# Layer 0 of a graph-attention chain: the sums' products grouped by four chunks, in written order

## The chip, the cores and the metric

The kernel runs on one core of a Trainium2 chip. The metric is the device time of one execution in microseconds (us); lower is better. TensorE multiplies matrices, VectorE and ScalarE work element by element, GpSimd (POOL) does one small reduction here, SyncE (SP) issues transfers. The engines run side by side and wait for each other by semaphores.

## The reference, cut to what matters

Four graph layers follow each other on `x` of 16 images (the batch) with 1024 nodes of 64 features, under one adjacency of 1024 x 1024; each ends in a residual and a layer norm. The change is in layer 0, a graph attention:

```python
def _L0_gnn_ref(h, W, a, adj):
    Wh = jnp.einsum('bni,io->bno', h, W)
    s1 = Wh @ a[:64, 0]
    s2 = Wh @ a[64:, 0]
    e = leaky_relu(s1[:, :, None] + s2[:, None, :], negative_slope=0.2)
    e = e + jnp.where(adj == 0, -1e9, 0.0)[None]
    attention = softmax(e, axis=2)
    h_prime = jnp.einsum('bnm,bmo->bno', attention, Wh)
    return elu(h_prime)
...
x = _layernorm(x + _L0_gnn_ref(x, L0_gnn_W, L0_gnn_a, adj))   # layer 0
x = _layernorm(x + _L1_gnn_ref(...))                          # layer 1: softmax of features over neighbours
x = _layernorm(x + _L2_gnn_ref(x, adj, ...))                  # layer 2: as layer 0, other weights
x = _layernorm(x + _L3_gnn_ref(x, adj, ...))                  # layer 3: four heads and an output head
```

## The kernel before

Layers 0 and 2 share one function, `gat_layer`. With `zero_mean` (layer 2) the features have no mean, 63 of them suffice, and the 64th column of the values is used for the softmax's sums. Layer 0's input isn't normalized, so all 64 columns are taken and the sums need products of their own.

The work on an image `b` is a loop over eight chunks `k` of 128 neighbours. `unit(k)` makes the tile `e` (128 neighbours x 1024 nodes, fp32) on VectorE in one instruction from `G`, `q` and the mask `aT`. `product(k, e)` multiplies on TensorE: two matrix products `y_l` with the values (`vals`, 64 columns each, one for each half of the nodes, side by side in the array), and in layer 0 also the sums `u_l` with `only`, a tile of 32 columns of which one is filled. The sums of two chunks make four products that lie side by side in the array; they are issued after every second chunk. `product` is issued two units behind `unit` (`LAG = 2`).

When an image's eight chunks are done, eight small tasks follow in the time of the next images, placed by slot (image, chunk): `evict` (ScalarE copies `yT`, `ysum` out of PSUM), `project` (TensorE, `po`, L1001 and L1005), `divide` (VectorE L1014 to L1019, then the exponential `m` on ScalarE, L1026), `residual` (VectorE L1031, L1032), `norm` (VectorE, eight `bn_stats`, L1040, and for an odd image the moments), `root`, `shift`, and `store` (ScalarE, eight scaled copies back into `x`, L775). Images go in pairs: `prep_x` (transposes `pxT`, L898), `prep_s` (`ps`, L904), `prep_top` (a maximum over all partitions on POOL), `prep_p`, `prep_G` (`pg` on TensorE, L939, then the exponential `G` on ScalarE, L940, one half of the nodes each) and `prep_v` make ready the next pair.

What sets the order of the instructions differs by layer. `gat_layer` has a flag `ordered`. Where it is true (layer 2), the engines' instructions stand in the order in which the code issues them. Where it is false (layer 0 before the change), a scheduler at build time chooses each engine's order from its own estimates, and may deal a task out between the units around it. [...] The flag is the last argument of the call:

```python
        extra = {(0, 6): [lambda: gat_setup(later["w2"], "l2", True)], (1, 6): [lambda: later["w3"]()]}
        ending = gat_layer(w_0, "l0", False, extra, first, 3, False)
```

`extra` holds setups of layers 2 and 3, which are done on the way through images 0 and 1 (weight transposes `wt`, products `l_pa`, `l_pw`, `pw`, and small copies on VectorE). `ending` are the tasks of the last images, which layer 1 takes over.

## Time and profile before

| what | us |
|---|---|
| median of 3 runs | 2162.24 (2161.66 to 2167.61) |
| the profiled execution, its own time | 2170.64 |
| its span, first to last instruction | 2168.8 |
| TensorE busy in the span | 2047.2 (94%) |
| VectorE busy | 1852.5 (85%) |
| ScalarE busy | 1227.5 (57%) |
| layer 0, first `y_l` to first `px` of layer 1 | 31.2 to 292.6 |
| one pair of images of layer 0, from `ps` to `ps` | 32.43 |
| layer 2, first `ps` to the start of layer 3 | about 471 to 735 |

All durations of single instructions come from the profiled execution. A row of a timeline gives start, length, engine, line, operation, tiles (out<-in), shape and how many instruction records follow each other. An fp32 matrix product leaves two records. The length runs to the modelled end of the last one; the start of the next row is the better measure of what a group costs. A bracket at the end is idle time of the engine just before, and what ended it. The granted clock is the share of TensorE's full clock over the stretch.

### The profile page before, as it was taken

What the parts mean: (1) busy time and instruction counts of PE and PEld (TensorE: products, weight loads), DVE (VectorE), ACT (ScalarE), POOL (GpSimd) and SP (SyncE); (2) the same over time, 40 slices, a digit from 0 to 9 for tenths busy, and PEclk for the clock granted to TensorE, in tenths of its full rate; (3) what the DMA queues carried; (4) which work ended last, traced back from release to release, by engine and by line L of the source; (5) the groups of instructions that cost most, each with busy time, mean ns of one, the idle gap of its engine ahead of it and who ended that gap; (6) DMA issues with size and microseconds to landing.
All of it is one profiled execution on the core that took longest, in us unless ns stands there. A gap on an engine that the chain in (4) does not pass through costs nothing.

```text
span 2168.8 us, 26641 instructions
## 1 busy us (share of the span) xinstructions
PE 2047.2 (94%) x10321; PEld 866.2 (40%) x10321; DVE 1852.5 (85%) x3221; ACT 1227.5 (57%) x1965; POOL 51.0 (2%) x77
## 2 busy tenths in 40 slices
PE   7999979998898899999999999999999999999993
PEld 3333347753433333333333333333333433343331
DVE  5888889978988877798898898889889889888997
ACT  4454556555535666566655665655665665565541
POOL 0000000000000000000000000000000000000001
PEclk8999989988978999999999999999999999999997
DMA  6000000000000200000000000000000000000000
GB/s 162 1 1 1 1 1 1 1 1 1 1 1 1 72 6 1 1 1 6 1 6 5 1 6 1 6 5 1 6 6 1 6 1 6 6 1 6 1 7 15
DMA packets 23656, 18.92 MB, mean 9 GB/s; under 512 B 19361, under 2 KB 19426, under 8 KB 23522
## 3 DMA queue, kind: packets, MB, share of 16 engines
q1 hardware_dynamic: 23218, 17.11, 2.8%
q8 instruction: 83, 1.36, 0.3%
q14 instruction: 51, 0.42, 0.1%
q10 hardware_dynamic: 304, 0.03, 0.0%
HBM read 12.95 MB, written 4.19 MB: 8 GB/s over the span
## 4 chain that ended last, share of the span: by engine, by line
PE 73%; DVE 21%; ACT 4%; issue 1%; DMA 0%; POOL 0%; SPq 0%; POOLq 0%; DVEq 0%; ACTq 0%
PE y L1259 18%; PE s L1247 17%; PE y_l L971 8%; PE s L1344 5%; PE y L1371 4%; DVE e L1252 4%; PE u_l L982 3%; DVE e L959 3%; PE po L1276 3%; PE po L1531 3%; PE po L1005 2%; PE pg L939 2%; PE po L1001 1%; PE ps L904 1%; ACT e L1251 1%
## 5 line engine op out<-in xcount | busy, mean ns | idle before, releaser
L1251 ACT ACTIVATE e<-s,shift 128x1024 f32<-128x1024 f32 x512 | 542.9, 1111 | 243.2 <-PE s L1247 237.8
L1252 DVE TENSOR_TENSOR e<-e,aT 128x1024 f32<-128x1024 f32 x512 | 602.6, 1220 | 87.7 <-ACT e L1251 85.6
L1247 PE MATMUL s<-hT 64*128 64x512 f32 x2048 | 509.9, 612 | 15.5 <-DVE top L1188 8.6
L1259 PE MATMUL y<-e,vals 128*64 128x512 f32 x2048 | 490.6, 601 | 3.2 <-ACT yT L1266 1.3
L959 DVE SCALAR_TENSOR_TENSOR e<-G_l,q,aT 128x1024 f32<-128x1024 f32 x256 | 319.9, 1276 | 20.5 <-ACT G_l L940 12.4
L971 PE MATMUL y_l<-e,vals_l 128*64 128x512 f32 x1024 | 278.8, 660 | 27.9 <-DVE e L959 26.3
L1247 PEld LDWEIGHTS s<-hT 64*128 64x128 f32 x2048 | 182.5, 186 | 256.0 <-issue 170.8
L1259 PEld LDWEIGHTS y<-e,vals 128*64 128x64 f32 x2048 | 131.0, 136 | 330.6 <-issue 258.0
L1349 ACT ACTIVATE e<-s,shift 128x1024 f32<-128x1024 f32 x128 | 141.8, 1113 | 85.1 <-PE s L1344 74.9
L1351 DVE TENSOR_TENSOR me<-e,aT 128x1024 f32<-128x1024 f32 x128 | 155.8, 1220 | 16.8 <-ACT e L1349 16.5
L1362 DVE SCALAR_TENSOR_TENSOR junk<-e,aN 128x1024 bf16<-128x1024 f32 x128 | 155.9, 1218 | 0.2
L1371 PE MATMUL y<-me,h2v 128*64 128x512 f32 x512 | 135.3, 609 | 10.5 <-DVE me L1351 10.4
L1344 PE MATMUL s<-h2T 64*128 64x512 f32 x512 | 136.3, 610 | 4.6 <-DVE h2v L1331 4.4
L971 PEld LDWEIGHTS y_l<-e,vals_l 128*64 128x64 f32 x1024 | 65.3, 146 | 184.9 <-issue 75.4
L1531 PE MATMUL po<-hi,aR 128*128 128x512 f32 x256 | 101.9, 398 | 2.7 <-ACT hi L1516 1.1
L775 ACT ACTIVATE x<-m,bn_shift,bn_rstd 128x64 f32<-128x64 f32 x256 | 88.7, 432 | 23.2 <-DVE bn_shift L766 23.2
L1531 PE MATMUL po<-lo,aR 128*128 128x512 f32 x256 | 99.8, 391 | 0.0
L1306 ACT COPY zT<-pzT 128x1024 f32<-128x1024 f32 x32 | 32.4, 1012 | 78.3 <-PE pzT L1305 78.3
L1276 PEld LDWEIGHTS po<-wb,yT 128*128 128x128 f32 x512 | 62.0, 190 | 34.0 <-issue 21.1
L1276 PE MATMUL po<-wb,yT 128*128 128x130 f32 x512 | 73.8, 287 | 1.3 <-ACT e L1251 1.2
L982 PE MATMUL u_l<-e,only 128*32 128x512 f32 x512 | 72.0, 612 | 0.0
L1344 PEld LDWEIGHTS s<-h2T 64*128 64x128 f32 x512 | 46.6, 186 | 63.7 <-issue 41.4
(214 smaller groups left out, 2019.9 us busy)
## 6 DMA issues: line engine op xcount, KB each, us to landing
adj<-in_adj_dram SPq DMA_DIRECT2D x16, 512.0 KB, 4.4
x<-in_x_dram SPq DMA_DIRECT2D x16, 256.0 KB, 5.0
out_dram<-res SPq DMA_DIRECT2D x16, 256.0 KB, 2.0
wl<-in_L_gnn_Wh_dram SPq DMA_DIRECT2D x2, 64.0 KB, 5.3
wo<-in_L_gnn_Wo_dram SPq DMA_DIRECT2D x1, 64.0 KB, 5.0
l_wd<-in_L_gnn_W_dram ACTq DMA_DIRECT2D x2, 16.0 KB, 4.7
l_wd<-in_L_gnn_W_dram SPq DMA_DIRECT2D x2, 16.0 KB, 2.0
bo<-in_L_gnn_bo_dram SPq DMA_DIRECT2D x1, 32.0 KB, 3.3
```

Source lines behind the costliest of these rows:

```text
L959: nc.vector.scalar_tensor_tensor(e, G[b - b % 2][:, b % 2, :], pq[b - b % 2][1][:, k, b % 2 : b % 2 + 1], aT[:, k, :], ALU.max, ALU.mult,)
L971: nc.tensor.matmul(held["y"][h * D : (h + 1) * D, :], vals[b][:, k, :], e[:, h * HALF : (h + 1) * HALF], start=(k == 0), stop=(k == C - 1),)
L1247: nc.tensor.matmul(s[:, i, :], hT[rows, k * P : (k + 1) * P], hT[rows, cols], start=True, stop=True)
L1251: nc.scalar.activation(e, s, AF.Exp, bias=shifts[b, n])
L1252: nc.vector.tensor_tensor(e, e, bc_mid(aT[:, k, cols], 2), ALU.mult)
L1259: nc.tensor.matmul(held[h][i * D : (i + 1) * D, :], vals[b][:, k, :], e[:, i, :], start=(k == 0), stop=(k == C - 1),)
L1276: nc.tensor.matmul(o[:, j // 2, j % 2, :], held["y"][:, c * P : (c + 1) * P], wb[:, n, :], start=True, stop=True,)
L1344: nc.tensor.matmul(s[:, i, :], hT[rows, (i + k // CH) % 2, k % CH * P : (k % CH + 1) * P], hT[rows, 0, :], start=True, stop=True,)
L1351: nc.vector.tensor_tensor(m, e, aT[:, k, :].rearrange("p (i q) -> p i q", i=2), ALU.mult)
L1362: nc.vector.scalar_tensor_tensor(junk, held.pop(k).rearrange("p i q -> p (i q)"), 1.0, aN[:, k, :], ALU.mult, ALU.mult, accum_out=sums[:, ...
L1371: nc.tensor.matmul(held["o"][h * D : (h + 1) * D, :], vals["out", b][:, k, :], e[:, h, :], start=(k == 0), stop=(k == C - 1),)
L1531: nc.tensor.matmul(po.rearrange("p q k f -> p (q k f)"), aR[:, k, ic * P : (ic + 1) * P], e[:, k].rearrange("p q k f -> p (q k f)"), start ...
```

## The change

In layer 0 alone: the sums' products wait until four chunks' products of values have been issued and then come as a group of eight; tiles `e` have ten buffers in place of seven; the small tasks have other slots (of an even image, `project`, `divide` and `residual` come two slots later, one for `residual`; of the next pair's preparation, `ps` and the second half of `G` come later, behind the sums), and the whole layer is recorded in written order. Layer 2 keeps its slots, and the other layers are untouched. No operation is added or left out.

```diff
-                e = pool.tile([P, N], F32, tag="e", name="e", bufs=7)
+                e = pool.tile([P, N], F32, tag="e", name="e", bufs=7 if zero_mean else 10)
...
-                if not zero_mean:
-                    if k % 2 == 0:
-                        held["e"] = e
-                    else:
-                        for r in range(4):
-                            kk, ee = (k - 1, held["e"]) if r < 2 else (k, e)
-                            h = r % 2
-                            nc.tensor.matmul(
-                                held["t"][r * 32 : (r + 1) * 32, :], only[b][:, kk, :],
-                                ee[:, h * HALF : (h + 1) * HALF], start=(kk < 2), stop=(kk >= C - 2),
-                            )
+                if zero_mean:
+                    return
+
+                held[k] = e
+                for kk in range(k - 3, k + 1) if k % 4 == 3 else ():
+                    ee = held.pop(kk)
+                    for h in range(2):
+                        r = kk % 2 * 2 + h
+                        nc.tensor.matmul(
+                            held["t"][r * 32 : (r + 1) * 32, :], only[b][:, kk, :],
+                            ee[:, h * HALF : (h + 1) * HALF], start=(kk < 2), stop=(kk >= C - 2),
+                        )
...
-            end = (3, 6) if b % 2 == 0 else (3, 2)
-            for task, (t, k) in zip(work[b][2], ((1, 1), (1, 3), (1, 4), (1, 6), (1, 7), (2, 0), (2, 2), end)):
+
+            places = [(1, 1), (1, 3), (1, 4), (1, 6), (1, 7), (2, 0), (2, 2), (3, 2) if b % 2 else (3, 6)]
+            if not zero_mean and b % 2 == 0:
+                places[1:4] = (1, 5), (1, 6), (1, 7)
+            for task, (t, k) in zip(work[b][2], places):
                 at(b + t, k, task)
...
+            if zero_mean:
+                places = (-2, 0), (-2, 1), (-2, 2), (-2, 3), (-1, 1), (-1, 2), (-1, 3), (-1, 4), (0, 4)
+            else:
+                places = (-2, 1), (-2, 1), (-2, 5), (-2, 6), (-1, 0), (-1, 1), (-1, 5), (-1, 4), (0, 4)
+            for task, (t, k) in zip(chain, places):
...
-        ending = gat_layer(w_0, "l0", False, extra, first, 3, False)
+        ending = gat_layer(w_0, "l0", False, extra, first, 3, True)
```

The nine places of the last list belong, in order, to the two halves of `prep_x`, `prep_s`, `prep_top`, `prep_p`, the two halves of `prep_G`, and `prep_v` of both images of the pair.

More of the change, by code (lines that the diff above doesn't have):

```diff
@@ L1072, in gat_layer @@
         for b in range(0, B, 2):
-            chain = [(lambda b=b, h=h: prep_x(b, h), -2, h) for h in range(2)]
-            chain += [(lambda b=b: prep_s(b), -2, 2), (lambda b=b: prep_top(b), -2, 3)]
-            chain += [(lambda b=b: prep_p(b), -1, 1)]
-            chain += [(lambda b=b, h=h: prep_G(b, h), -1, 2 + h) for h in range(2)]
-            chain += [(lambda b=b: prep_v(b), -1, 4), (lambda b=b: prep_v(b + 1), 0, 4)]
-            for task, t, k in chain:
+            chain = [
+                lambda b=b: prep_x(b, 0), lambda b=b: prep_x(b, 1), lambda b=b: prep_s(b), lambda b=b: prep_top(b),
+                lambda b=b: prep_p(b), lambda b=b: prep_G(b, 0), lambda b=b: prep_G(b, 1),
+                lambda b=b: prep_v(b), lambda b=b: prep_v(b + 1),
+            ]
+            if zero_mean:
[3 more added lines that the diff above has]
+            for task, (t, k) in zip(chain, places):
                 if b + t < 0:
```

## Prediction

> **What bounds the kernel now.** I read the page's busy shares first, then the stretches of layer 0 and layer 2, then TensorE's timeline in one pair of images, then ScalarE's and VectorE's. Layer 0's products run from 31.2 us (first y_l) to 292.6 us (first px of layer 1): 261.4 us of the span. The busy times by stretch (stretch, its length, busy us of each engine, granted clock):

> ```profile
> core 0: us, PE busy (x) PEld busy (x) DVE busy (x) ACT busy (x) POOL busy (x), PEclk, DMA share, GB/s
> 138.38:170.80 32.42, 32.42 (x209) 11.96 (x209) 27.14 (x60) 16.80 (x48) 0.35 (x1) 1.00 0.00 1
> 470.00:735.00 265.00, 236.59 (x1168) 104.46 (x1166) 222.95 (x472) 132.91 (x382) 9.34 (x9) 0.83 0.02 7
> ```

> The first row is one pair of images of layer 0: TensorE has no hole in 32.42 us and full clock, VectorE has 5.3 us spare. Five pairs follow each other at 32.43 us. The second is layer 2, recorded in written order already: TensorE is idle 11% of it and its granted clock is 0.83. TensorE's timeline inside the pair (start, length, line, records; two records are one matmul):

> ```profile
> 152.80 1.08 PE L971 MATMUL y_l<-e,vals_l 128*64 128x512 f32 x4
> 153.81 1.13 PE L939 MATMUL pg<-xT_l,l_w 64*128 64x512 f32 x4
> 154.87 1.08 PE L971 MATMUL y_l<-e,vals_l 128*64 128x512 f32 x4
> 155.88 1.06 PE L982 MATMUL u_l<-e,only 128*32 128x512 f32 x8
> 156.87 1.05 PE L1001 MATMUL po<-l_ind,ysum_l 128*128 128x2 f32 x8
> 157.86 1.11 PE L1005 MATMUL po<-l_wd,yT_l 64*128 64x64 f32 x16
> 158.80 1.08 PE L939 MATMUL pg<-xT_l,l_w 64*128 64x512 f32 x4
> 159.81 1.94 PE L971 MATMUL y_l<-e,vals_l 128*64 128x512 f32 x8
> 161.68 1.06 PE L982 MATMUL u_l<-e,only 128*32 128x512 f32 x8
> ```

> From start to start: values of two chunks (y x8) 1.87 us, of one chunk (y x4) 1.01, sums of two chunks (u x8) 1.00. A chunk more in a y group therefore costs 0.86, and cutting a group costs 2 x 1.01 - 1.87 = 0.15. ScalarE at the same place:

> ```profile
> 159.49 1.10 ACT L775 ACTIVATE x<-m,bn_shift,bn_rstd 128x64 f32<-128x64 f32 x3 [3.00 <-DVE bn_shift L766]
> 160.50 1.09 ACT L940 ACTIVATE G_l<-pg,up 128x1024 f32<-128x1024 f32 x1
> 161.50 0.62 ACT L1026 ACTIVATE m<-v 128x512 f32<-128x512 f32 x1
> 162.02 4.41 ACT L775 ACTIVATE x<-m,bn_shift,bn_rstd 128x64 f32<-128x64 f32 x13
> ```

> After G, the exponential of divide (m) goes ahead of 13 of the 16 stores; a store takes 0.33 from start to start. And VectorE:

> ```profile
> 161.63 1.28 DVE L959 SCALAR_TENSOR_TENSOR e<-G_l,q,aT 128x1024 f32<-128x1024 f32 x1 [1.43 <-ACT G_l L940]
> 162.83 0.68 DVE L1031 SCALAR_TENSOR_TENSOR v<-v,x 128x512 f32<-128x512 f32 x1
> 163.43 1.28 DVE L959 SCALAR_TENSOR_TENSOR e<-G_l,q,aT 128x1024 f32<-128x1024 f32 x1
> ```

> The scheduler deals the residual out between the next image's e tiles; an e takes 1.195 from start to start.

> [...]

> **The change, part by part.** Times below are of TensorE unless another engine is named.

> 1. Sums behind four chunks. Before, four chunks cost 2 x (1.867 + 0.996) = 5.73. After: y of four chunks 1.009 + 3 x 0.859 = 3.59, sums 0.996 + 0.859 = 1.86 (that a second set of sums costs 0.86 like a chunk of y is taken; at worst 1.00). Saved 0.285 per four chunks, 32 times: **9.1**.

> 2. Small tasks behind sums. In the built order a pair reads: pxT, y of 2, po, y of 2, u, ps, y of 4, u, pg | y of 4, u, po, pg, y of 4, u. One cut of y is left where there were three, and pxT is whole (its halves took 0.586 and 0.585; some 1.02 together). That is 0.45 per pair over six pairs: **2.7**. A pair without waits is 32.43 - 4 x 0.285 - 0.45 = 30.84. Both together save **11.8**.

> 3. Written order. No instruction is added, and no DMA: SP's and POOL's work keeps its order; only vector, scalar and matrix instructions move. What they stand behind now is the question. At the end of an odd image t (images t-1 and t are a pair) VectorE has: divide of t-1, e(7) of t, residual and norm of t-1, then e(0) of the next pair. ScalarE has: second half of G, **eight stores of image t-3, then** the exponential that this residual needs. G waits for pg, which stands behind po. Nothing of e(0) can start before. From the moment that pg starts:
>  - pg until G can start 1.12 (1.01 to the next group, 0.11 to its end and the signal)
>  - G to the next on ScalarE 1.00
>  - eight stores 8 x 0.333 = 2.66
>  - exponential 0.62, signal 0.04
>  - residual, two steps of 0.685 with 0.04 each 1.45; eight bn_stats 1.02
>  - e(0) 1.28, signal 0.05

>  Behind the waiting residual VectorE has norm and e(0) to e(4), for which y(0) to y(4) wait; behind the late exponential ScalarE has the copies yT and ysum, read by po only two chunks later, so they delay nothing.

>  Sum 9.24. In the meantime TensorE has pg 1.01, y of 4 3.59, u 1.86, pxT 1.02 = 7.48. It then **stands 1.76**. Then y(1) follows e(1), 1.195 behind instead of 0.86 (0.34), and the last y of the next odd group waits 0.15 and is cut (0.15), because norm and moments stand ahead of its e on VectorE. Per pair 2.40: 30.84 + 2.40 = 33.2 against 32.43. Such boundaries: after images 3, 5, 7, 9, 11. After 13 there is no pxT to cover, so 1.02 more. After image 1 no store exists yet: 9.24 - 2.66 = 6.58 is under 7.48, no wait. Sum 5 x 2.40 + 3.42 = **15.4**.

> 4. Setups and ends. Layer 2's weights (wt, l_pa, l_pw) and layer 3's (wt, pw) now stand in order between products; l_pw waits for some ten small vector steps of 0.06 to 0.28, and e(5) behind the copies to wb waits too: 2.0 and 1.5, by adding those steps; from 1 to 5 together. The first four products of image 0 follow e at 1.195: 3 x 0.34 = 1.0. In image 15 VectorE has 8 x 1.195 + divide 1.2 + residual and norm 2.5 + moments 1.3 = 14.6, TensorE 2 x 5.44 + po 2.0 = 12.9: some 1.6. Sum **6.1**.

> 5. Three more e tiles hide nothing here: VectorE doesn't wait for a tile at the boundary but for the exponential. Priced at nothing; they are needed so that four chunks can be held.

> Without a change of clock: 15.4 + 6.1 - 11.8 = **9.7 longer**. Everything behind layer 0 stands in the same order, so nothing pays it back.

> 6. Clock. [...] Bounds: 0, and layer 2's loss (0.17 of the clock over a pair's 33 is 5.6, of which its vector-bound stretches hide part; I take 3 per pair, 20 in all).

> Forecast: **+13.7**. The profiled execution took 2170.64 (span 2168.8), 8.4 above the median of 2162.24; the sum gives 2184.3 against it and **2176** against the median.

> **The rivals.**
>  - R1, faster: the stand doesn't form. It decides if the chain is under 7.48, thus 1.8 shorter, as it would be if the stores were through before pg lands. For it: ScalarE is busy only 16.80 of 32.42. Against: the stores stand behind G in a queue in order. Then items 1 and 2 less the setups and ends (6.1, or half that): -6 to -9, 2153 to 2156.
>  - R2, about the same: waits half as long and no loss of clock: +9.7 - 7 = about +3, 2165. For it: each term of the chain is small, and TensorE's ends are modelled. Against: all durations are measured, and the stand is a difference of two sums that share no large guess.
>  - R3, slower by more: every boundary loses the clock as layer 2 does: +9.7 + 18, 2190. For it: clock 0.83 there. Against: layer 2 has more and other holes.
>  - R4, the grouped sums cost no less than two groups: 0.14 x 32 = 4.4 of the saving goes. But between pg and e(0) the chain sets the time, so about a third of it is hidden: +3, within the range.

> **How the numbers follow.** About 0.3% (6.5 us) is what a measurement of this kernel can tell from no change. Forecast with R3 and R4: 0.76. R2: 0.13. R1: 0.11. So slower 0.76, same 0.13, faster 0.11. The range from 2162 to 2190 leaves out R1 and the far end of R3.

> **What would show it.** Right: u_l in groups of 16 records, 1.86 from start to start; pairs at 33 to 35 us; at each of six boundaries a hole of 1.5 to 3 us ahead of y_l, ended by VectorE's e; VectorE idle some 3 us ahead of L1032 (residual, new number), put down to ScalarE's m; stores x8 between G and m; clock of layer 0 under 1.00. Wrong: pairs at 31 us with TensorE full, or no idle time ahead of the residual. If pairs are at 33.2 and the clock stays 1.00, item 6 falls and the rest stands.

## The result, and the profile after

The changed kernel takes **2177.42 us** (median of 6 runs, 2173.56 to 2180.48) against 2162.30 (6 runs, 2159.52 to 2167.61) for the kernel before, run beside it: ratio 1.0064, 95% interval 1.0048 to 1.008. That is slower by more than the 0.3% that can be told from no change. Its profiled execution took 2178.10 us, its span 2176.3.

Layer 0 takes 274.84 us from its first `y_l` to the first `px` of layer 1, where it took 261.39: **13.45 more**. Nothing behind it changed its order. The two profiled executions differ by only 7.5 us, because layer 2 took 261.7 us in this one and 270.8 in the one before, both from its first `ps` to the first product `s` of layer 3. (By these marks layer 2 before lies at 457.3 to 728.1 us. The stretch from about 470 to 735 that stands for it ahead of the result starts 13 us late and runs 7 us into layer 3; its clock is 0.83 by both.) A difference of that size needs no change: two profiled executions of one and the same kernel (e3_scheduled and e12_scheduled_beside below) gave 261.9 and 269.5 for layer 2. So layer 0 is compared by its own stretch here, and kernels by their medians.

Stretches of the changed kernel (stretch, length, busy us of PE, PEld, DVE, ACT, POOL, granted clock, DMA share, GB/s): layer 0, then two pairs of images from `ps` to `ps`, in the second of which the clock falls too, then layer 2.

```profile
32.40:307.24 274.84, 256.17 (x1613) 102.00 (x1614) 224.66 (x483) 119.14 (x344) 7.92 (x7) 0.96 0.04 8
105.63:139.06 33.43, 31.33 (x210) 12.84 (x211) 28.09 (x60) 16.68 (x49) 1.31 (x1) 1.00 0.00 1
139.00:175.61 36.61, 34.52 (x208) 14.74 (x209) 28.17 (x60) 16.67 (x49) 1.23 (x1) 0.91 0.00 1
474.00:735.70 261.70, 229.66 (x1178) 101.07 (x1178) 224.70 (x482) 133.82 (x392) 9.71 (x10) 0.86 0.02 7
```

In the pair before the change TensorE was busy for all of 32.42 us. Now it is busy for 31.33 and stands (has nothing to do) for 2.1 in a pair of 33.43. The second pair has the same work and the same stands; its granted clock is 0.91 and it is 3.17 longer.

The timeline of the changed kernel at the end of an odd image, all engines mixed (start, length, engine, line, operation, tiles, records, and in brackets the idle time before and what ended it):

```profile
129.67 1.08 PE L939 MATMUL pg<-xT_l,l_w 64*128 64x512 f32 x4
...
130.68 3.65 PE L971 MATMUL y_l<-e,vals_l 128*64 128x512 f32 x16
130.80 1.12 ACT L940 ACTIVATE G_l<-pg,up 128x1024 f32<-128x1024 f32 x1 [5.66 <-PE pg L939]
...
131.81 2.75 ACT L775 ACTIVATE x<-m,bn_shift,bn_rstd 128x64 f32<-128x64 f32 x8
...
134.27 1.92 PE L983 MATMUL u_l<-e,only 128*32 128x512 f32 x16
134.46 0.62 ACT L1027 ACTIVATE m<-v 128x512 f32<-128x512 f32 x1
...
135.11 0.69 DVE L1032 SCALAR_TENSOR_TENSOR v<-v,x 128x512 f32<-128x512 f32 x1 [2.85 <-ACT m L1027]
...
136.12 1.09 PE L898 MATMUL pxT<-ident,x 128*128 128x128 f32 x8
...
136.57 1.11 DVE L1041 BATCH_NORM_STATS2 bn<-m 128x6 f32<-128x64 f32 x8
...
137.59 6.06 DVE L959 SCALAR_TENSOR_TENSOR e<-G_l,q,aT 128x1024 f32<-128x1024 f32 x5
...
139.01 2.82 PE L971 MATMUL y_l<-e,vals_l 128*64 128x512 f32 x8 [1.80 <-DVE e L959]
```

Read it by engine. On ScalarE the eight stores (L775) come between `G` and the exponential `m`; before, `m` came first. VectorE stands 2.85 us until `m` is there, and residual (L1032, and L1033 behind it), norm (L1041) and then the five `e` follow in its order. TensorE runs out of work at 137.2 and stands 1.80 until the first of these `e`. The waits of layer 0, from 42 us on, show the same two by their sums (us in total, times, longest):

```profile
DVE v L1032 <- ACT m L1027: 17.1, 6, 2.9
PE y_l L971 <- DVE e L959: 14.7, 14, 2.8
```

### The profile page after: what moved, and what is told of

Its sections match the earlier page's. It is cut to its first block, busy times and chain, and to the rows that moved or that the text cites. A ratio compares the mean times of both kernels' runs of the same rounds, so it can differ in the third digit from the quotient of the medians.

```text
span 2176.3 us, 26690 instructions
## 1 busy us (share of the span) xinstructions
PE 2035.8 (94%) x10321; PEld 871.0 (40%) x10321; DVE 1860.7 (86%) x3221; ACT 1227.2 (56%) x1965; POOL 55.4 (3%) x77
## 4 chain that ended last, share of the span: by engine, by line
PE 66%; DVE 25%; ACT 6%; issue 1%; DMA 0%; SPq 0%; POOL 0%; POOLq 0%; DVEq 0%; ACTq 0%
PE y L1267 18%; PE s L1255 17%; DVE e L959 5%; PE y_l L971 5%; PE s L1352 5%; PE y L1379 4%; DVE e L1260 4%; PE po L1284 3%; PE po L1539 3%; PE po L1006 2%; PE u_l L983 2%; PE po L1002 1%; ACT x L775 1%; PE ps L904 1%; DVE bn L1041 1%
## 5 line engine op out<-in xcount | busy, mean ns | idle before, releaser
L959 DVE SCALAR_TENSOR_TENSOR e<-G_l,q,aT 128x1024 f32<-128x1024 f32 x256 | 315.8, 1279 | 7.1 <-ACT G_l L940 5.5
L971 PE MATMUL y_l<-e,vals_l 128*64 128x512 f32 x1024 | 274.5, 664 | 42.7 <-DVE e L959 40.4
L971 PEld LDWEIGHTS y_l<-e,vals_l 128*64 128x64 f32 x1024 | 69.2, 148 | 199.6 <-issue 99.8
L775 ACT ACTIVATE x<-m,bn_shift,bn_rstd 128x64 f32<-128x64 f32 x256 | 88.5, 434 | 2.7 <-DVE bn_shift L766 2.7
L940 ACT ACTIVATE G_l<-pg,up 128x1024 f32<-128x1024 f32 x32 | 35.7, 1116 | 70.7 <-PE pg L939 70.0
```

Source lines behind the costliest of these rows:

```text
L959: nc.vector.scalar_tensor_tensor(e, G[b - b % 2][:, b % 2, :], pq[b - b % 2][1][:, k, b % 2 : b % 2 + 1], aT[:, k, :], ALU.max, ALU.mult,)
L971: nc.tensor.matmul(held["y"][h * D : (h + 1) * D, :], vals[b][:, k, :], e[:, h * HALF : (h + 1) * HALF], start=(k == 0), stop=(k == C - 1),)
```

## The experiments

All are timed beside the kernel before. "Pair" is the length from `ps` to `ps` in the middle of layer 0 where the granted clock is 1.00 ("warm"), "layer 0" its stretch as above, "stand" that of TensorE ahead of the first `y_l` behind an odd image. Layer 0, pair and stand are read from one profiled execution of each kernel.

| kernel | median (range, runs) | ratio to before, 95% | layer 0 | pair | stand at the boundary |
|---|---|---|---|---|---|
| changed kernel | 2177.42 (2173.56 to 2180.48, 6) | 1.0048 to 1.008 | 274.84 | 33.44 | 1.80 |
| e1_store_behind | 2163.37 (2158.44 to 2169.03, 12) | 0.9986 to 1.0014 | 257.02 | 31.24 | 0 |
| e2_half_stores | 2167.92 (2161.6 to 2172.86, 20) | 1.0011 to 1.0029 | 262.55 | 32.11 | 0.47 |
| e3_scheduled | 2155.92 (2154.39 to 2158.8, 9) | 0.9954 to 0.9975 | 251.29 | 30.82 | 0 |
| e4_old_in_order | 2175.41 (2172.2 to 2176.87, 5) | 1.0033 to 1.0066 | 272.78 | 33.42 | 0.92, behind an even image |
| e5_residual_later | 2164.53 (2160.34 to 2167.79, 20) | 1.0 to 1.0016 | 255.92 | 31.24 | 0 |
| e6_sums_by_two | 2176.82 (2175.12 to 2188.33, 5) | 1.0046 to 1.009 | 274.18 | 33.74 | 1.51 |
| e7_group_only | 2173.15 (2169.92 to 2177.24, 5) | 1.0036 to 1.0073 | 268.24 | 31.85 | 0 |
| e8_setups_apart | 2158.29 (2153.07 to 2166.43, 20) | 0.9971 to 0.999 | 251.90 | 31.24 | 0 |
| e9_best | 2154.71 (2150.42 to 2159.92, 11) | 0.9939 to 0.9971 | 247.76 | 30.82 | 0 |
| e10_narrow_filler | 2209.22 (2206.35 to 2214.55, 4) | 1.0178 to 1.0243 | 298.07 | none warm | 0 |
| e11_wide_filler | 2181.04 (2179.48 to 2184.88, 4) | 1.005 to 1.0111 | 276.56 | 34.67 | 0 |
| e12_scheduled_beside | 2157.18 (2152.55 to 2167.46, 14) | 0.996 to 0.999 | 251.54 | 30.82 | 0 |

### Is it the stores ahead of the exponential?

**e1_store_behind** puts an even image's stores one slot later, behind `m`:

```diff
             if not zero_mean and b % 2 == 0:
                 places[1:4] = (1, 5), (1, 6), (1, 7)
+                places[7] = (3, 7)
```

> The changed kernel with one slot moved: the store of an even image goes from (3, 6) to (3, 7), so that on ScalarE the exponential of divide stands ahead of the eight stores. Theory A (the eight stores ahead of the exponential make the hole at the end of each pair): the chain from pg to e(0) loses 8 x 0.333 = 2.66 and is 6.6, under TensorE's 7.5; the 1.80 hole ahead of y_l goes, VectorE no longer waits 2.8 for ScalarE's m, a pair takes 31.2 in place of 33.44, and 15 to 20 us come back, clock included: 2158 to 2163, about level with the kernel before or a little under it. Theory B (tiles e held for four chunks starve VectorE): nothing changes, 2177. Theory C (written order costs by itself, whatever the stores): the hole stays or moves to another wait, 2172 or more.

The timeline at the same boundary:

```profile
129.00 0.62 ACT L1027 ACTIVATE m<-v 128x512 f32<-128x512 f32 x1
129.52 2.74 ACT L775 ACTIVATE x<-m,bn_shift,bn_rstd 128x64 f32<-128x64 f32 x8
129.65 0.69 DVE L1032 SCALAR_TENSOR_TENSOR v<-v,x 128x512 f32<-128x512 f32 x1 [0.20 <-ACT m L1027]
...
132.13 6.06 DVE L959 SCALAR_TENSOR_TENSOR e<-G_l,q,aT 128x1024 f32<-128x1024 f32 x5
...
134.33 1.94 PE L971 MATMUL y_l<-e,vals_l 128*64 128x512 f32 x8
```

`m` stands ahead of the stores again, the residual waits 0.20 in place of 2.85, and `y_l` has no bracket: TensorE goes on from `pxT` without a stand. One slot for one task takes 17.8 us out of layer 0 and 14 out of the time, which is 0.4 above the top of what was expected. No operation differs.

**e2_half_stores** leaves four stores ahead and puts four behind:

```diff
...
+            tasks = list(work[b][2])
+            if not zero_mean and b % 2 == 0:
+                store = tasks.pop()
+                tasks += [lambda store=store: store(range(CH)), lambda store=store: store(range(CH, C))]
+                places.append((3, 7))
...
```

> The changed kernel with the store of an even image in two tasks: four of its eight scaled copies stay in slot (3, 6), ahead of the exponential, four go to (3, 7), behind it. Theory A: the chain is shorter by 4 x 0.333 = 1.33, so the hole of 1.80 shrinks to about 0.47 and a pair from 33.44 to about 32.0; the time lies between the changed kernel and the one with all stores behind, 2166 to 2170. Theories B and C: the hole is as long as before, 2177.

The stand is 0.47 at five boundaries and 1.49 at the last, which has no `pxT` to cover it: four stores fewer, 4 x 0.333 = 1.33, from 1.80 and from 2.83. So the stand here is a difference of two lengths, and not a fixed toll for a wait.

**e5_residual_later** leaves all eight stores ahead, but takes the residual and the norm out from in front of the `e` tiles:

```diff
-                places[1:4] = (1, 5), (1, 6), (1, 7)
+                places[1:5] = (1, 5), (1, 6), (2, 1), (2, 2)
```

> The changed kernel with the stores left ahead of the exponential, but the residual and the norm of an even image placed behind e(1) and e(2) of the next pair (slots (2, 1) and (2, 2) in place of (1, 7) and (1, 7)). Theory A, sharpened: the late exponential costs only because e(0) stands behind the residual on VectorE. Then the hole ahead of y_l goes here too: a pair of 31.2, about as the run with the stores behind, 2161 to 2165. Rival: it is ScalarE's lateness itself that holds TensorE (its copies yT and ysum, or G); then the hole stays at some 1.8, 2175 or more.

The pair is 31.24, and there is no stand at the five boundaries between such pairs. So the stores do harm only because VectorE's `e` tiles are queued behind an instruction that waits for `m`. Either end of the chain may be cut.

### Is it the order, or the grouping?

**e3_scheduled** is the changed kernel with the scheduler in layer 0, **e4_old_in_order** the kernel before in written order. The edit of e3_scheduled (e4_old_in_order sets the same flag of the kernel before from False to True):

```diff
-        ending = gat_layer(w_0, "l0", False, extra, first, 3, True)
+        ending = gat_layer(w_0, "l0", False, extra, first, 3, False)
```

> The changed kernel with the flag of layer 0 false again: sums grouped by four, ten tiles e and the new slots stay, the order is the scheduler's. Theory A: TensorE is full, a pair takes 32.43 - 4 x 0.285 - 0.45 = 30.85, layer 0's clock is 1.00 and no setup waits: 2150 to 2154, 8 to 12 under the kernel before. Theory B: e tiles run out, TensorE has holes, 2165 or more. Theory C: as A.

> The kernel before with only the flag of layer 0 set true: sums grouped by two, seven tiles e, old slots, written order. Its stores stand behind the exponential (divide in slot 4, store in slot 6 of the same image). Theory A: no hole of 1.8 ended by the residual's wait; what is left are the setups and ends of the prediction (about 6) and more cuts of y_l by small tasks (at 0.15 each, some four per pair more), so about +6 to +9 on the kernel before, 2168 to 2172. Theory C: the written order makes holes as in the changed kernel, with pairs of 34 and the clock falling in layer 0, 2180 or more. Theory B: without grouping no loss, 2162.

With the scheduler, the new grouping and slots give a pair of 30.82 without a stand and a time below both kernels, though 2 us above the top of what was expected: layer 0 is 10.1 shorter than before.

Written order alone costs the kernel before 11.4 us of layer 0, more than I had expected (2175.41 us for 2168 to 2172). Its pair is 33.42, with a stand of 0.92 ahead of a `y_l`, the first one behind an even image:

```profile
124.72 2.48 DVE L959 SCALAR_TENSOR_TENSOR e<-G_l,q,aT 128x1024 f32<-128x1024 f32 x2
125.46 0.59 ACT L993 COPY ysum_l<-u_l 128x512 f32<-128x512 f32 x1
126.15 1.08 PE L971 MATMUL y_l<-e,vals_l 128*64 128x512 f32 x4 [0.93 <-ACT ysum_l L993]
```

This `y_l` waits for VectorE and for ScalarE. At 123.83 to 124.72 us VectorE has the small steps of an odd image's moments, 0.89 in all, and the first `e` stands behind them and ends at 126.00. On ScalarE the first step of `root` (L702) waits 4.09 us for the same moments, and the copies yT and `ysum` stand behind it; `ysum` ends at 126.05, and the profile puts the stand down to it. The two ends lie 0.05 apart, so which of them alone would make the stand was not separated. Both are late behind the moments. I had not foreseen that stand.

**e6_sums_by_two** is the changed kernel with the sums' products after every second chunk:

```diff
-                for kk in range(k - 3, k + 1) if k % 4 == 3 else ():
+                for kk in range(k - 1, k + 1) if k % 2 else ():
```

> The changed kernel with the sums grouped by two chunks again, all else kept. Theory A: of the four groups of a pair three lose their 0.285, the fourth lies under the chain and is hidden: TensorE's cover is 7.76, the hole 1.5, a pair 33.44 + 0.86 = 34.3, or less where y_l waits for e anyway (34 at the least): 2180 to 2184. Theory B (grouping starves VectorE): the hole goes, 2168 or less.

The stand is shorter, 1.51, because TensorE has 0.285 more work to cover the same chain, and the pair is 0.30 longer than in the changed kernel. I had expected 34 at the least, and 2180 to 2184 for the 2176.82 measured. In written order, then, grouping saves 0.30 of the 1.14 per pair that its products give. Of the rest, about 0.5 goes into stands (2.11 per pair in the changed kernel, 1.63 here); where the remainder goes was not followed. In the profile layer 0 is even 0.7 shorter than in the changed kernel, with the clock at half for 10.2 us of it in place of 22.9.

**e7_group_only** is the kernel before with the sums grouped by four and ten `e` tiles, with the old slots and the scheduler:

```diff
-                e = pool.tile([P, N], F32, tag="e", name="e", bufs=7)
+                e = pool.tile([P, N], F32, tag="e", name="e", bufs=7 if zero_mean else 10)
...
+                for kk in range(k - 3, k + 1) if k % 4 == 3 else ():
...
```

> The kernel before with the grouping by four and the ten tiles e alone; old slots, the scheduler's order. Item 1 of the prediction alone: 32 x 0.285 = 9.1 of layer 0's 261.4, a pair 32.43 - 1.14 = 31.3: 2153 to 2156, 1 to 3 slower than with the new slots under the scheduler. Rival: grouping costs what it saves (VectorE waits for tiles), 2162.

I had expected 2153 to 2156; it took 2173.15, some 18 us more. One part is the pair: 31.85 warm, where 31.3 was expected. At the old slots the small tasks still cut the groups of `y_l`, of which a warm pair has nine (eleven before, five in e3_scheduled). The larger part is the clock: TensorE has no hole in all of layer 0, and yet its clock fell to half four times, for 6.83 us each. Its stretches at one fall, and TensorE's timeline across it:

```profile
110.43:113.84 3.41, 3.41 (x22) 2.52 (x23) 1.85 (x5) 0.00 (x0) 0.35 (x1) 1.00 0.00 0
113.84:120.67 6.83, 6.83 (x24) 2.25 (x27) 2.28 (x7) 3.03 (x12) 0.00 (x0) 0.50 0.01 2
```

```profile
107.46 1.95 PE L904 MATMUL ps<-l_w,xT_l 128*128 128x4 f32 x16
109.34 1.08 PE L971 MATMUL y_l<-e,vals_l 128*64 128x512 f32 x4
110.35 1.05 PE L1002 MATMUL po<-l_ind,ysum_l 128*128 128x2 f32 x8
111.33 1.10 PE L1006 MATMUL po<-l_wd,yT_l 64*128 64x64 f32 x8
112.36 1.07 PE L971 MATMUL y_l<-e,vals_l 128*64 128x512 f32 x2
113.37 1.56 PE L1006 MATMUL po<-l_wd,yT_l 64*128 64x64 f32 x8
```

The window of 3.41 us ahead of the fall is 100% busy. But most of it is `po`, whose products stream 2 or 64 columns (the last number of the shape) where a `y_l` streams 512. The group of sums no longer stands between `ps` and `po`, as it did before the change.

### What makes the clock fall?

In the profiles of before and after the granted clock is 1.00 or 0.50, and every stretch of half clock lasts a whole multiple of 3.41 us (3.41 to 17.07; only the last, which the trace's end cuts off, doesn't). For each window of that grid I worked out from the timeline what share of it TensorE spent streaming columns (512 columns of a record counted as 0.43 us, half of the 0.86 that a chunk of `y_l` takes, fewer columns in proportion; products side by side once). These shares are estimates. In these two profiles, from 30 us on, 35 falls to half clock came behind shares of 0 to 0.59, 32 of them behind 0.44 or less; the 1133 windows of full clock with no fall behind them had 0.37 or more. From 0.37 to 0.59 both occur; so too in e7_group_only, where the window ahead of the fall has 0.44, and the one before that, with 0.38, was followed by full clock. That is an argument from traces, so two kernels test it. Both are e8_setups_apart (below) with filler ahead of the products of `ps`, of equal length (3.59 and 3.54 us in the traces): sixteen products of 128x4, or four of 128x512. The listing has both edits; each kernel has the one that bears its name:

```diff
             pt = ps_t.tile([P, HALF], F32, tag="t", name="ps12")
+            for c in range(0 if zero_mean else 2 * C):        # e10_narrow_filler
+                c %= C
+                nc.tensor.matmul(
+                    pt[:, 4 * c : 4 * c + 4], xT[b][:, c * P : (c + 1) * P], w4, start=True, stop=True
+                )
+            for c in range(0 if zero_mean else 4):            # e11_wide_filler
+                nc.tensor.matmul(pt, xT[b][:, c * P : (c + 1) * P], xT[b][:, :HALF], start=True, stop=True)
```

> e8_setups_apart with the eight products of `ps` (128x4) of layer 0 issued three times over, with the same result: TensorE is busy for 2 x 1.74 = 3.48 us more in each pair, without a stand, but streams hardly any columns meanwhile. Work alone: 8 x 3.48 = 27.8, layer 0 251.9 + 7 x 3.48 = 276.3, time about 2186. Theory A (the clock falls after a window of 3.41 us in which TensorE streams few columns, whether it stands or not): the stretch of 5.2 us of such products always fills most of one window, so the clock falls to half behind each of the seven `ps` slots inside layer 0, for one or two windows, 1.3 to 3.2 us each: layer 0 285 to 299, time 2194 to 2209. Theory B (the clock falls after stands, time in which TensorE has nothing to do): no more falls than in e8_setups_apart, layer 0 276, time 2184 to 2188.

> The control to e10_narrow_filler: e8_setups_apart with four products of 128x512 in the place where e10_narrow_filler has sixteen of 128x4, same tiles read, same PSUM tile written, and nothing of it read afterwards. About the same time on TensorE (four times about 0.9, half of a group of four pairs of `y_l` at 3.58 each pair 0.9: 3.6 us per pair of images), but with full streaming. Both theories: no fall of the clock at the `ps` slots, layer 0 251.9 + 7 x 3.6 = 277, time 2184 to 2189. If the falls in e10_narrow_filler come from the longer boundary alone (later `e` tiles, VectorE, buffers) and not from the columns, they come here too, and the two kernels take the same time, over 2194.

TensorE's timeline at one `ps`, first with the narrow filler:

```profile
162.62 3.74 PE L908 MATMUL ps<-l_w,xT_l 128*128 128x4 f32 x32
166.21 2.73 PE L912 MATMUL ps<-l_w,xT_l 128*128 128x4 f32 x16
168.87 6.16 PE L979 MATMUL y_l<-e,vals_l 128*64 128x512 f32 x16
```

The stretches of one window of 3.41 us in it and of the whole pair that follows (columns as above):

```profile
163.72:167.13 3.41, 3.41 (x33) 3.41 (x32) 0.19 (x1) 0.00 (x0) 0.00 (x0) 1.00 0.00 0
162.62:200.32 37.70, 37.70 (x244) 17.87 (x240) 28.16 (x60) 16.88 (x49) 1.23 (x1) 0.91 0.00 1
```

and the pair with the wide one:

```profile
149.81:184.47 34.66, 34.47 (x218) 14.39 (x217) 28.17 (x59) 16.68 (x48) 1.23 (x1) 1.00 0.00 1
```

With narrow products TensorE is busy for all 37.70 us and has clock 0.91: the `y_l` group behind takes 6.16 in place of 3.65. The window from 163.72 to 167.13 us is 100% busy at full clock and streams columns for 0.03 of its time by the estimate above; at 167.13 the clock fell to half. It fell at all seven `ps` slots inside layer 0. With wide products TensorE even stands 0.19, and the clock stays 1.00; no `ps` slot has a fall. The mean granted clock of the two profiled executions is 0.954 and 0.968. The two kernels differ by 28.2 us (in the profiles 21.5 in layer 0, and 6.4 ahead of its first `y_l`, where the first `ps` lies) for fillers of the same length. So idle time alone doesn't tell where the clock falls: in the pair with none of it the clock is 0.91 (narrow), in the pair with 0.19 us of it 1.00 (wide). The theory of stands fails here. The fillers differ in their number of products and of weight loads too (32 records against 8), which these runs don't separate from the columns. e10_narrow_filler came out 0.2 above the top of its expectation, as all seven falls last two windows or three; e11_wide_filler 3 below its own.

### The rest, and a faster version

**e8_setups_apart** is e1_store_behind with the setups of layers 2 and 3 cut into steps, given to nine slots in place of two (`step(i)` issues the next step of one setup; the cuts inside the setups are left out here):

```diff
-        extra = {(0, 6): [lambda: gat_setup(later["w2"], "l2", True)], (1, 6): [lambda: later["w3"]()]}
+        extra = {p: [lambda: step(0)] for p in ((0, 4), (0, 5), (0, 6), (0, 7))}
+        extra.update({p: [lambda: step(1)] for p in ((1, 1), (1, 2), (1, 3), (1, 5), (1, 6))})
```

> The run with the stores behind the exponential, and the setups of layers 2 and 3 in four and five steps, each in a slot of its own ((0, 4) to (0, 7), and (1, 1), (1, 2), (1, 3), (1, 5), (1, 6)), so that no product stands behind a chain of small vector steps. Item 4: the holes of 0.38, 1.90, 0.28 and 0.73 in the first pair go, 3.3 of layer 0[...]: layer 0 from 257.0 to 251 to 254, the time 2156 to 2160. Rival: image 0 is paced by e there, and the setups cost nothing, 2163.

As expected: of the setups' stands (0.38, 1.90, 0.28, 0.73) one of 0.13 is left, a `y_l` behind them waits 0.47 for its `e`, and layer 0 is 5.1 shorter. **e9_best** adds a later place for the odd images' norm, root and shift:

```diff
+            if not zero_mean and b % 2:
+                places[4:7] = (2, 3), (2, 4), (2, 5)
```

> e8_setups_apart (layer 0 in written order, the even image's stores behind the `ps` slot, the setups in steps) with one step more: an odd image's `norm`, `root` and `shift` come in the slots (2, 3), (2, 4), (2, 5) in place of (1, 7), (2, 0), (2, 2), so that they stand apart from the next unit's `e` tiles. Theory (in written order a stand of TensorE is work queued ahead of an `e` tile on VectorE or ScalarE): the stands of 0.19 before the fourth `y_l` group of an odd image go, a pair falls from 31.24 to about 30.9, layer 0 from 251.9 to 249 to 251, and the time to 2152 to 2157. Rival (those stands are given back somewhere else, or 31.24 is what TensorE needs): pair 31.2, layer 0 252, time 2157 to 2160.

> e3_scheduled once more (the changed kernel with the scheduler in place of the written order in layer 0), on the chip of e9_best, to see which of the two is ahead. Expected 2155.9 as before (2154 to 2159), layer 0 251.3, pair 30.82, no stand; e9_best about the same or up to 3 us faster if its shorter layer 0 is real, since everything behind layer 0 is alike.

Layer 0 of e9_best, and one pair:

```profile
105.40:136.23 30.83, 30.83 (x213) 12.94 (x209) 28.19 (x60) 16.91 (x49) 1.31 (x1) 1.00 0.00 1
30.35:278.11 247.76, 246.36 (x1613) 99.25 (x1614) 224.14 (x483) 120.23 (x344) 7.91 (x7) 0.99 0.05 10
```

TensorE has no hole in the pair, as before the change, but the pair is 1.6 shorter. Both versions beat both kernels: e9_best 2154.71, e12_scheduled_beside 2157.18 on the same chip, with intervals that overlap. e9_best's layer 0 is 3.8 shorter than that of e12_scheduled_beside; in the time that lead isn't told apart from nothing.

## Why the prediction was right, point by point

The forecast of 2176 met 2177.42. The mechanism of the largest term, the chain at the boundary, is the one that was forecast; the 4 us counted for the clock were my own estimate, which no trace of the kernel before showed.

- **Items 1 and 2, saved products.** A group of `u_l` has 16 records and takes 1.854 from start to start (1.86 predicted), `y_l` x16 3.584 (3.59), `pxT` x8 1.023 (1.02). A pair without stands, predicted at 30.84, is 30.82 in e3_scheduled and e9_best. R4 is out. But e7_group_only shows that item 1 doesn't stand by itself: without the new slots a warm pair gains 0.58 of its 1.14. And over the whole of layer 0 the two items were put at 11.8, while e3_scheduled, which has them without written order, is 10.1 shorter than the kernel before, even with no half clock in its layer 0 (10.2 us before).
- **Item 3, the chain at the boundary.** By its terms, predicted and (from the timeline) measured: `pg` to `G` 1.12, 1.13; `G` 1.00, 1.01; stores 2.66, 2.65; `m` 0.66, 0.65; residual 1.45, 1.46; norm 1.02, 1.02; `e` until `y_l` 1.33, 1.42. In all 9.24, 9.34. The stand of 1.76 is 1.80 in the trace, five times; after image 13 2.83 (2.78 predicted); after image 1 none. A pair was put at 33.2 and is 33.44 at full clock. e1_store_behind, e2_half_stores and e5_residual_later show the two links, stores and residual, each by itself: without either no stand, with half the stores 0.47. R1, no stand, is out.
- **Item 4, setups and ends.** The setups' stands are 0.38 + 1.90 and 0.28 + 0.73, thus 2.3 and 1.0 for 2.0 and 1.5. e8_setups_apart takes 5.1 out of layer 0, more than these stands: the clock was at half for 13.8 us of layer 0 with the setups together and for 5.8 with them apart, and item 6 counts the clock. The ends weren't tried apart. In the trace image 15 has stands of 1.42 for the 1.6 of the item; the first four products of image 0 take 4.75 for 3.59, 1.2 where 1.0 was put down to `e`, but the clock is at half there until 34.8 us.
- **Item 5, ten `e` tiles.** Priced at nothing, and nothing contradicts it: VectorE waits at the boundary for `m`. More or fewer tiles weren't tried.
- **Item 6, the clock.** The forecast of 13.7 is 9.7 without a change of clock and 4 for the clock. These 4 were my own estimate, and that they came out near is luck. Half clock followed three of the six boundaries and two setups. A fall of a single window cost 1.30 (pair 34.74 against 33.44), one that lasted two windows 3.17 (pair 36.61, outside the 33 to 35 foretold). Half clock lasts 22.9 us of layer 0 against 10.2 before; 12.7 more at 1.30 for 3.41 or 3.17 for 6.83 is 4.8 to 5.9, an estimate and at most, for the 4 of the item. The length of a stand doesn't tell where the clock falls: five of the six stands have the same 1.80, and the clock fell at two of them and held at three; e7_group_only has no stand, and its clock fell four times. The share of streaming in the poorest window at each of the six boundaries is, by the estimate, 0.42, 0.38, 0.53, 0.44, 0.39 and 0.32; the clock fell behind 0.38, 0.39 and 0.32. The profile's busy time doesn't tell it either, since a window that is 100% busy by it (e10_narrow_filler, 163.72 to 167.13 us) was followed by half clock; its share of streaming is 0.03.
- **The sum.** Layer 0 is 13.45 longer for a predicted 13.7. That it is so close is luck in part: items 1 and 2 gave 10.1 (by e3_scheduled) for 11.8, and written order cost 23.5 (274.84 against 251.29) where items 3, 4 and 6 add up to 25.5; the two misses cancel. Set against the profiled execution, the sum was 2184.3, and that execution took 2178.10; layer 2's 9 us lie between, a difference such as two profiles of one kernel also show.

R2 (half the waits, 2165) fell with the stand of 1.80. R3 (clock lost at every boundary, 2190) needed all six boundaries, and at three the clock held.

What stays open: what decides between shares of 0.37 and 0.59, and why layer 2 takes 262 us in one profiled execution and 269 in another of the same kernel. Layer 2 is at half clock for 75 us of the first and 92 of the second; in the profiles of after and before, where it takes 261.7 and 270.8, for 71.7 and 92.2. Why its clock differs was not shown.

## What to carry to other kernels

In written order the residual, 2.85 us late by its input `m`, held up the norm and the five `e` behind it on VectorE, and TensorE stood 1.80 for them; in e1_store_behind and e5_residual_later it did not. So put work that nobody waits for (here the stores) behind what the next stage waits for, and a step that waits (here the residual) behind the tiles that don't need it. Size such a stand as a difference: the chain of the engines that are queued, less the work that the bounding engine has meanwhile (9.24 - 7.48 = 1.76 for the 1.80 measured). Before small products are moved together, look at what streams in each 3.41 us of TensorE: in e7_group_only, where no group of sums lay between `ps` and `po` any more, the clock fell four times, for 6.83 us each.
